# Graph sum and expert layers on one core: whole jobs behind a pair's sums, more scratch banks, biases in SBUF

## The chip, the core and the metric

The kernel runs on one core of a Trainium2 chip, in fp32. The metric is the time of one execution on the device in microseconds, as the median of several. Before the change the median of three runs is 2438.28 us (2429.11 to 2442.33).

## What is computed

The inputs are 12500 nodes of 256 features, and 200000 edges, each with a source, a destination and a weight, sorted by destination. Destinations are drawn as 12500 u^2, so low node numbers get many more edges than high ones.

```python
def _L0_gnn_ref(X, edge_src, edge_dst, edge_val, W, b):
    support = X @ W
    msgs = support[edge_src] * edge_val[:, None]
    out = jax.ops.segment_sum(msgs, edge_dst, num_segments=N_NODES)
    return out + b
...
h = jax.nn.gelu(jnp.einsum('nd,edf->enf', xf, W1) + b1[:, None, :], approximate=False)
y = jnp.einsum('enf,efd->end', h, W2) + b2[:, None, :]
out = jnp.einsum('ne,end->nd', w_dense, y)
out = _layer_norm(out + x, gamma, beta)
...
x = x + _L0_gnn_ref(_layernorm(x, axis=-1), src, dst, edge_weight, L0_gnn_W, L0_gnn_b)
x = x + _L0_ffn_ref(_layernorm(x, axis=-1)[None], L0_ffn_Wr, L0_ffn_br, L0_ffn_W1, L0_ffn_b1, L0_ffn_W2, L0_ffn_b2, L0_ffn_gamma, L0_ffn_beta)[0]
```

The router's logits come from the mean of the normalised rows over all tokens. So one softmax picks two of eight experts for the whole graph, with 256 x 512 and 512 x 256 weights each.

## The kernel before

**Start (0 to 96 us).** Rows of x are normalised and written to a DRAM table xn. The accumulator acc, which holds the summed messages of all nodes with features on the partitions, is cleared in SBUF.

**The pair loop (L898 to L933).** Edges are cut into chunks of 128 and these into groups of four. A pair is two such groups: eight chunks, 1024 edges. The loop runs over 180 pairs from high node numbers to low ones. For each pair:

- `gather_pair` (L480) issues eight indirect DMAs from POOL, one a chunk; each brings 128 rows of xn into a tile g. There are three such tiles. The gathers of pair i+1 are issued in iteration i, behind its products.
- `multiply` (L494) has a small TensorE product (L502) that waits for the gathers, and eight products of a chunk's rows with a weighted selection of 32 columns (L507). They fill one PSUM bank, pt; its pool has one. ACT copies it to SBUF, part (L510).
- `spread_out` (L515) runs one pair later: four products per pair (L522, two per group) put the sums of 32 columns on their places within a window of nodes, into the one bank ps, and DVE adds each group into acc at a place read from memory (L541).
- `select` (L437) makes the selections on DVE: for the first pairs in three instructions with two SBUF inputs (L462, L468, L472), later with a scalar form (L448).
- `prepare_segment` (L314) now and then turns the edges of the next segment into columns and places, with a few row products (L335).

**Dense part.** The first 128 chunks, those of the lowest nodes, are not gathered. In the pairs 1 to 44 `dense_make` (L602) makes two one-hot matrices for each of three chunks a pair on DVE, and `dense_add` (L612) multiplies them on TensorE (L620): products of one lot (four chunks, later two) sum up in one PSUM bank dps, then DVE adds the lot into a matrix inside acc (L634). There are 44 lots, and dps has one bank. Then `multiply_tiles` (L656) multiplies this matrix with xn, read in large tiles, in the same bank across nine pairs (L662); `place_dense` (L666) and `clear_matrix` (L675) put the result in place.

**Node blocks.** When all edges of a block of 256 nodes are in, `product` (L722) adds the graph's bias to the rows of x (L726, DVE), multiplies acc by W (L730, bank gz), adds both (L731) and takes the statistics; one pair later ACT normalises (L745), the next pair `transposed` (L754) transposes the rows (L759, again bank gz), ACT copies them out (L763), and DVE adds the last bias beta to acc (L768); then they are stored (`keep`). There are 49 blocks. Both biases lie in a PSUM bank of their own, bias_ps, filled at the start by a matmul (L297).

**Jobs.** A block and one of the two experts make a job, 98 in all. The first expert is named when 24 blocks are through, the second at 38. `job_steps` (L842) cuts a job: four first products (`first` L819, two matmuls of L822 each, into one of two banks ph, with Gelu by ACT L823) and two second products (`second` L825, four matmuls of L830 each, bank po, moved out by DVE L836). After every second `first` comes one `second` of the job before. `work` (L869) takes steps while a budget is above zero; a first costs 0.88, a second 1.75, and the budget of a pair starts from 10.0 - 2.5 - 1.0 (L915 to L918):

```python
budget = min(budget, 0.0) + PAIR_US - OWN_US - SLACK_US
budget -= 1.9 * complete + 1.3 * (stage_t is not None)
if i + 1 < len(pairs):
    budget = work(budget)
```

The order on every engine is that of the program, written by hand: on TensorE in one iteration the segment's rows, the pair's sums, the spread of the pair before, the dense steps, the job steps, transposes, product. On ACT the copy of the sums stands ahead of the Gelus of its iteration.

**Tail (2265 to 2447 us).** The last two jobs, then the two experts' outputs are mixed on TensorE (L1027, L1028), added and normalised for 25 double blocks. Mixes rotate through banks (`banks` L1009): three of their own, gz, the bias bank, and, when no jobs are left, ph and po.

Of the kernel before, what the change touches and what calls it, by code (L numbers as in the profile page):

```python
# [10 lines left out]
FP = mybir.dt.float32  # L11
# [3 lines left out]
ALU = mybir.AluOpType  # L15
# [3 lines left out]
P = 128  # L19
# [33 lines left out]
MARGIN = 8  # L53

PAIR_US = 10.0
OWN_US = 2.5
SLACK_US = 1.0

# [49 lines left out]
def gnn_ffn_kernel(  # L108
# [154 lines left out]
    jobs_stack, stack = ExitStack(), ExitStack()  # L263
    with tc.tile_pool(name="rt", bufs=1) as rt, tc.tile_pool(
        name="bias_ps", bufs=1, space=bass.MemoryType.PSUM
    ) as biasp, jobs_stack, stack, tc.manual_schedule():

# [13 lines left out]
        sp = open_pool(jobs_stack, name="small", bufs=4)  # L281
        gps, hps, ops = psum("gz_ps", 1, jobs_stack), psum("h_ps", 2, jobs_stack), psum("o_ps", 1, jobs_stack)

# [7 lines left out]

        bias_ps = biasp.tile([P, 2, D], FP, name="bias_ps")
        with tc.tile_pool(name="once", bufs=1) as once:
            bias_row = once.tile([1, 2, D], FP, name="bias_row")
            nc.scalar.dma_start(bias_row[:, 0], b_gnn[None, :])
            nc.scalar.dma_start(bias_row[:, 1], beta[None, :])
            nc.tensor.matmul(  # L297
                bias_ps.rearrange("p k d -> p (k d)"), row, bias_row.rearrange("p k d -> p (k d)"), start=True, stop=True
            )
        edgep = open_pool(name="edges", bufs=2)  # L300
# [118 lines left out]
        xp = open_pool(name="xrows", bufs=2)  # L419
        pps, aps, dps = psum("part_ps", 1), psum("agg_ps", 1), psum("dense_ps", 1)  # L420
        dp = open_pool(name="dense", bufs=1)
# [72 lines left out]
        def multiply(i, g):  # L494

            n = pairs[i][1]
            sel = selections[i][0]
            pt = pps.tile([P, GB, D], FP, name="pt")
            part = partp.tile([P, GB, D], FP, name="part")


            nc.tensor.matmul(  # L502
                pt[:NARROW, 0, : n * SUPER], sel[:, n * SUPER - 1], g[:, : n * SUPER, 0], start=True, stop=True
            )
            for j in range(n * SUPER):
                q = slice(j % SUPER * NARROW, (j % SUPER + 1) * NARROW)
                nc.tensor.matmul(  # L507
                    pt[q, j // SUPER], sel[:, j], g[:, j], start=True, stop=True, tile_position=(0, j % SUPER * NARROW)
                )
            nc.scalar.activation(part[:, :n], pt[:, :n], AF.Copy)  # L510
            return part

# [41 lines left out]
        dense_w = dp.tile([P, DENSE_CHUNKS], FP, name="dense_w")  # L554
        lot_i = dp.tile([1, len(lots)], I32, name="lot_i")

        def prepare_dense():
# [53 lines left out]

        def dense_add(c):  # L612

            g = next(g for g, (c0, k) in enumerate(lots) if c0 <= c < c0 + k)
            c0, k = lots[g]
            if c == c0:
                made["ps"] = dps.tile([P, 2 * D], FP, name="dps")
            ps = made["ps"][:, :QW]
            r, q = made.pop(c)
            nc.tensor.matmul(ps, r, q, start=(c == c0), stop=(c == c0 + k - 1))  # L620
            if c == c0 + k - 1:
# [12 lines left out]
                nc.vector.tensor_tensor(  # L634
                    at, at, ps.rearrange("p (h q n) -> p h q n", h=H, n=DENSE_WIN), ALU.add
                )
# [18 lines left out]

        def multiply_tiles(k):  # L656
            if k == 0:
                made["sum"] = dps.tile([P, 2 * D], FP, name="dps")
            for q in range(4 * k, min(4 * k + 4, NQ)):
                m = min(P, N - q * P)  # L660
                h, at = divmod(q, QH)
                nc.tensor.matmul(  # L662
                    made["sum"][:DENSE, :D], matrix[:m, h, at], loaded[k][:m, q % 4], start=(q == 0), stop=(q == NQ - 1)
                )

        def place_dense():  # L666

            by_node = w2_flat[:DENSE, :D]
            nc.scalar.activation(by_node, made["sum"][:DENSE, :D], AF.Copy)
            ps = dps.tile([P, H, 2 * P], FP, name="dps")  # L670
            for h in range(H):
                nc.tensor.transpose(ps[:, h, :DENSE], by_node[:, h * P : (h + 1) * P], ident[:DENSE, :DENSE])
            made["ps"] = ps

        def clear_matrix(i, n):  # L675
            w = QH * DENSE // n
            nc.vector.memset(acc[:, :, i * w : (i + 1) * w], 0.0)
            if i == 0:
                nc.scalar.activation(acc[:, :, :DENSE], made["ps"][:, :, :DENSE], AF.Copy)

        made_to = [0, 0]

        def dense_steps(i):

            if i == 0:
                prepare_dense()
                return
            while made_to[1] < made_to[0]:
                dense_add(made_to[1])
                made_to[1] += 1  # L690
            while made_to[0] < min(DENSE_CHUNKS, DENSE_STEP * i):
# [6 lines left out]
            if 0 <= k and ROWS_STEP * k < NLOAD:  # L698
                for j in range(ROWS_STEP * k, min(NLOAD, ROWS_STEP * k + ROWS_STEP)):
                    multiply_tiles(j)  # L700
                    load_tiles()
            if i == dense_pairs - 1:
                place_dense()
            if dense_pairs <= i < dense_pairs + 4:
# [49 lines left out]
        def transposed(b, z):  # L754

            ps = gps.tile([P, H, TB], FP, name="gz")
            for j in range(TPB):
# [8 lines left out]
            at = nodes(b * TPB, TPB)  # L766
            last_bias = halves(bias_ps[:, 1]).unsqueeze(1).to_broadcast([P, TPB, H, P])
            nc.vector.tensor_tensor(at, at, last_bias, ALU.add)  # L768
# [73 lines left out]
        def job_steps():  # L842

            while True:
                fetch()
                if not at_hand:
                    if behind:
                        yield 1.75, behind.pop(0)
                    else:
                        yield None  # L850
                    continue
                k, b, zT = at_hand.pop(0)
                fetch()
                hT = hp.tile([P, FC, TB], FP, name="hT")
                job_open[0] = True
                for c in range(FC):
                    yield 0.88, lambda c=c: first(k, zT, hT, c)
                    if c % 2 and behind:
                        yield 1.75, behind.pop(0)
                made = {}  # L860
                job_open[0] = False
                behind.extend(
                    [lambda h=h, a=(k, b, zT, hT, made): second(*a, h) for h in range(H)]
                )

        steps = job_steps()
        ready, named = [], 0

        def work(budget):  # L869

            while budget > 0:
                step = next(steps)
                if step is None:
                    break
                step[1]()
                budget -= step[0]
            return budget

# [19 lines left out]
        for i, (s0, n) in enumerate(pairs):  # L898
            k, at = seg_of(s0)
            since = 0 if at + n == segs[k][1] else since + 1  # L900
            if k + 1 < NSEG:
                if since == 0 and k > 0:
                    load_segment(k + 1)
                if since == 4:
                    prepare_segment(k + 1)
            part = multiply(i, g)
            if i + 1 < len(pairs):
# [101 lines left out]
        def banks():  # L1009
# [323 lines left out]
```

## Time and profile before

| what | value |
|---|---|
| median of three runs | 2438.28 us |
| profiled execution, its time | 2448.85 us |
| its span | 2446.9 us |
| granted TensorE clock, mean | 0.876 |
| TensorE busy | 1718.6 us, 70% |
| DVE busy | 1190.5 us, 49% |
| ACT busy | 475.8 us, 19% |
| POOL busy | 1488.0 us, 61% |
| gathers (L486) | 1436, 953 ns each |
| stretches | 0 to 96 start, 96 to 892 pairs with the dense part, 892 to 2265 pairs with jobs, 2265 to 2447 tail |

A line of the groups reads: line, engine, operation, output tile <- input tiles, size, count, then busy time and mean of one in ns, then the idle time of the engine just ahead of such instructions and what ended it. A line of a timeline reads: start in us, duration, engine, line, operation, tiles, count, and in brackets the idle time before it and its releaser. "issue" means that the trace shows nothing that it waited for, "remote" that the releaser is not known. PE is TensorE and PEld its weight loads. Matmul ends are modelled. The stretches above come from the table of engines by stretch.

### The profile page before, as it was taken

How to read it: one execution, taken by the hardware profiler on the slowest of the kernel's cores; microseconds unless marked ns; L12 is line 12 of the kernel's file. 1: busy time of each engine (PE TensorE's matmuls, PEld its weight loads, DVE VectorE, ACT ScalarE, POOL GpSimd, SP SyncE). 2: the span in 40 equal slices, each digit the busy share in tenths (PEclk: the TensorE clock that was granted, in tenths of full speed). 3: DMA queues.
4: the chain of work that ended last, by engine and by line, in shares of the span. 5: the costliest groups of instructions: out<-in, count | busy, mean ns of one | idle time of the engine just before them, and what ended most of it. 6: DMA issues, size and time to landing. Idle time of an engine off the chain costs nothing.

```text
span 2446.9 us, 29786 instructions
## 1 busy us (share of the span) xinstructions
PE 1718.6 (70%) x9698; PEld 1215.8 (50%) x9698; DVE 1190.5 (49%) x4265; ACT 475.8 (19%) x1085; POOL 1488.0 (61%) x1537
## 2 busy tenths in 40 slices
PE   0056655666567468888888878888887888888775
PEld 0033333333344246656656656566565665565675
DVE  7355555655533544545444444434433433343688
ACT  5201101111101122212122112212121211211233
POOL 5666656665565666666666666666666666665144
PEclk9987767877788779999999989999998999989898
DMA  8533333332375344444444454444444444444486
GB/s 304 193 91 116 103 93 102 109 114 83 116 225 167 110 145 142 136 138 139 141 131 135 138 151 144 133 134 141 133 136 125 137 137 134 130 123 120 160 281 219
DMA packets 167602, 349.17 MB, mean 143 GB/s; under 512 B 33514, under 2 KB 77072, under 8 KB 167440
## 3 DMA queue, kind: packets, MB, share of 16 engines
q0 software_dynamic: 68928, 188.31, 27.2%
q1 hardware_dynamic: 94120, 145.65, 17.6%
q10 hardware_dynamic: 4392, 13.21, 1.4%
q8 instruction: 82, 1.34, 0.2%
q14 instruction: 80, 0.66, 0.1%
HBM read 282.91 MB, written 64.14 MB: 142 GB/s over the span
## 4 chain that ended last, share of the span: by engine, by line
PE 48%; another core or an unknown queue 17%; DVE 16%; issue 12%; ACT 4%; DMA 2%; POOL 1%; SPq 0%; ACTq 0%; DVEq 0%; POOLq 0%
PE ph L822 14%; PE po L830 12%; PE ps L522 5%; PE pt L507 5%; PE dps L620 4%; PE gz L730 3%; DVE st L69 2%; PE dps L662 2%; DVE acc L541 1%; ACT hT L823 1%; ACT xt L393 1%; ACT part L510 1%; DVE nmt L1052 1%; DVE w L609 1%
## 5 line engine op out<-in xcount | busy, mean ns | idle before, releaser
L486 POOL DMA_INDIRECT g<-xn,src_i x1436 | 1368.3, 953 | 810.4 <-issue 394.2
L822 PE MATMUL ph<-zTj,w 128*128 128x256 f32 x1568 | 452.0, 420 | 127.5 <-issue 55.0
L830 PE MATMUL po<-hT,w 128*128 128x256 f32 x1568 | 438.3, 412 | 105.9 <-issue 80.9
L541 DVE TENSOR_TENSOR acc<-acc,ps 128x256 f32 x359 | 151.0, 421 | 678.8 <-remote 293.2
L822 PEld LDWEIGHTS ph<-zTj,w 128*128 128x128 f32 x1568 | 309.9, 208 | 229.0 <-issue 101.7
L830 PEld LDWEIGHTS po<-hT,w 128*128 128x128 f32 x1568 | 314.8, 206 | 197.6 <-issue 125.7
L510 ACT ACTIVATE part<-pt 128x512 f32<-128x512 f32 (+1 forms) x180 | 107.2, 596 | 1145.2 <-remote 596.2
L620 PE MATMUL dps<-w 128*128 128x490 f32 x256 | 151.5, 718 | 146.3 <-DVE acc L634 113.7
L823 ACT ACTIVATE hT<-ph,b 128x256 f32<-128x256 f32 x392 | 178.6, 472 | 311.2 <-PE ph L822 173.2
L448 DVE TENSOR_SCALAR sel<-iota,rel,wgt 128x32 f32<-128x32 f32 x992 | 233.4, 319 | 0.0
L522 PEld LDWEIGHTS ps<-spread,part 128*128 128x128 f32 x1436 | 186.8, 203 | 93.6 <-issue 87.0
L522 PE MATMUL ps<-spread,part 128*128 128x128 f32 x1436 | 223.3, 301 | 11.4 <-DVE acc L541 8.8
L507 PE MATMUL pt<-g,sel 128*32 128x256 f32 x2872 | 219.9, 418 | 0.0
L836 DVE SCALAR_TENSOR_TENSOR yT<-po,b,zTj 128x256 f32<-128x256 f32 x196 | 85.7, 479 | 163.1 <-PE po L830 73.5
L730 PE MATMUL gz<-wg,acc 128*128 128x256 f32 x392 | 120.0, 460 | 49.0 <-remote 15.2
L620 PEld LDWEIGHTS dps<-w 128*128 128x128 f32 x256 | 52.5, 232 | 203.6 <-DVE acc L634 133.8
L502 PE MATMUL pt<-g,sel 128*32 128x8 f32 (+1 forms) x360 | 42.4, 190 | 131.3 <-DMA g<-xn,src_i 71.6
L502 PEld LDWEIGHTS pt<-g,sel 128*32 128x32 f32 x360 | 26.2, 113 | 204.1 <-issue 165.2
L730 PEld LDWEIGHTS gz<-wg,acc 128*128 128x128 f32 x392 | 89.3, 233 | 74.3 <-issue 37.1
L731 DVE TENSOR_TENSOR acc<-gz,xt 128x512 f32<-128x512 f32 x49 | 33.9, 691 | 167.7 <-PE gz L730 107.1
L507 PEld LDWEIGHTS pt<-g,sel 128*32 128x32 f32 x2872 | 98.7, 118 | 26.2 <-issue 8.8
L1044 POOL TENSOR_TENSOR rst<-vet,half 128x4 f32<-128x4 f32 (+1 forms) x25 | 42.4, 1697 | 108.4 <-DVE vet L1042 108.4
(183 smaller groups left out, 1586.6 us busy)
## 6 DMA issues: line engine op xcount, KB each, us to landing
zTj<-zts SPq DMA_DIRECT2D x98, 256.0 KB
yts<-yT SPq DMA_DIRECT2D x98, 256.0 KB
ab<-yts SPq DMA_DIRECT2D x48, 512.0 KB
g<-xn,src_i POOLq DMA_INDIRECT x1436
zts<-zT SPq DMA_DIRECT2D x49, 256.0 KB
xt<-in_x SPq DMA_DIRECT2D x24, 512.0 KB
xn<-xt ACTq DMA_DIRECT2D x24, 512.0 KB
xt<-in_x SPq DMA_DIRECT2D x48, 256.0 KB
```

The lines of the kernel that those rows point to most:

```text
L448: nc.vector.tensor_scalar(sel[:, j * SUPER + c], iota[:, :NARROW], t["rel"][:, col], t["wgt"][:, col], ALU.is_equal, ALU.mult,)
L486: nc.gpsimd.indirect_dma_start(out=g[:, j], out_offset=None, in_=xn, in_offset=bass.IndirectOffsetOnAxis(ap=segment[k]["src_i"][:, col : c ...
L507: nc.tensor.matmul(pt[q, j // SUPER], sel[:, j], g[:, j], start=True, stop=True, tile_position=(0, j % SUPER * NARROW))
L510: nc.scalar.activation(part[:, :n], pt[:, :n], AF.Copy)
L522: nc.tensor.matmul(ps[:, j, h], part[:, j, h * P : (h + 1) * P], spread[:, j], start=True, stop=True)
L541: nc.vector.tensor_tensor(at, at, ps[:, j], ALU.add)
L620: nc.tensor.matmul(ps, r, q, start=(c == c0), stop=(c == c0 + k - 1))
L730: nc.tensor.matmul(ps[:, j], node_tile(t0 + j)[:, h], wg[:, h], start=(h == 0), stop=(h == H - 1))
L822: nc.tensor.matmul(ph, w1[:, k, h, c * P : (c + 1) * P], zT[:, h], start=(h == 0), stop=(h == H - 1))
L823: nc.scalar.activation(hT[:, c], ph, AF.Gelu, bias=b1[:, k, c : c + 1])
L830: nc.tensor.matmul(po[:, h], w2[:, k, c, h * P : (h + 1) * P], hT[:, c], start=(c == 0), stop=(c == FC - 1))
L836: nc.vector.scalar_tensor_tensor(yT[:, i], po[:, i], b2[:, k, i : i + 1], zT[:, i], op0=ALU.add, op1=ALU.add)
```

## The change

Six things are edited:

1. The copy of the sums leaves `multiply` and becomes `hand_over`, which is called behind the pair's job steps. Everything between is unchanged in order, so ACT now has the Gelus of an iteration ahead of its copy.
2. A pair gets a whole job or none: `work` starts one only with a budget above 3.5, and then does all of it. The seconds of the job before come first, then the four firsts. The budget is carried on unclipped, at 10.0 - 2.4 - 0.8 a pair.
3. The scratch pool h_ps has four banks in place of two. The bias bank and the dense bank are given up.
4. `dense_add` takes the chunks of a pair: the part of a lot that falls in a pair is summed in a scratch bank and added by DVE at once. This makes 72 pieces of 44 lots. `multiply_tiles` likewise sums one pair's tiles in a scratch bank, and DVE copies or adds it to an SBUF tile by_node. The transpose moves from `place_dense` to the first step of `clear_matrix`. Block transposes use a scratch bank as well.
5. The biases lie in an SBUF tile, loaded by two broadcasting DMAs on ACT's queue; L726 and L768 read it in place of PSUM.
6. The tail's mixes have two banks of their own, and the rotation uses scratch banks where the third and the bias bank were.

Both kernels do 384 first and 192 second products within the pair loop (96 jobs) and two jobs behind it. In the changed order about 97 of the pairs 62 to 177 have a whole job behind their sums and some 20 have none.

```diff
 PAIR_US = 10.0
-OWN_US = 2.5
-SLACK_US = 1.0
+OWN_US = 2.4
+SLACK_US = 0.8
+JOB_US = 3.5
...
-        gps, hps, ops = psum("gz_ps", 1, jobs_stack), psum("h_ps", 2, jobs_stack), psum("o_ps", 1, jobs_stack)
+        gps, hps, ops = psum("gz_ps", 1, jobs_stack), psum("h_ps", 4, jobs_stack), psum("o_ps", 1, jobs_stack)
...
+        biases = rt.tile([P, 2, D], FP, name="biases")
+        for k, v in enumerate((b_gnn, beta)):
+            nc.scalar.dma_start(biases[:, k], bass.AP(tensor=v.tensor, offset=v.offset, ap=[[0, P], [1, D]]))
...
-        pps, aps, dps = psum("part_ps", 1), psum("agg_ps", 1), psum("dense_ps", 1)
+        pps, aps = psum("part_ps", 1), psum("agg_ps", 1)
...
+            return part, pt
+
+        def hand_over(i, part, pt):
+            n = pairs[i][1]
             nc.scalar.activation(part[:, :n], pt[:, :n], AF.Copy)
-            return part
...
+        def dense_add(c0, c1):
+
+            for g, (a, k) in enumerate(lots):
+                b0, b1 = max(a, c0), min(a + k, c1)
+                if b0 >= b1:
+                    continue
+                ps = scratch_ps()[:, :QW]
+                for c in range(b0, b1):
+                    r, q = made.pop(c)
+                    nc.tensor.matmul(ps, r, q, start=(c == b0), stop=(c == b1 - 1))
...
-            nc.vector.tensor_tensor(xt, xt, bias_ps[:, 0].unsqueeze(1).to_broadcast([P, TPB, D]), ALU.add)
+            nc.vector.tensor_tensor(xt, xt, biases[:, 0].unsqueeze(1).to_broadcast([P, TPB, D]), ALU.add)
...
-            ps = gps.tile([P, H, TB], FP, name="gz")
+            ps = scratch_ps().rearrange("p (h t) -> p h t", h=H)
...
+                while behind:
+                    yield 1.75, behind.pop(0), False
                 for c in range(FC):
...
+                    yield 0.88, lambda c=c: first(k, zT, hT, c), c == FC - 1
...
-            while budget > 0:
+            while budget > least:
...
+                while least and not step[2]:
+                    step = next(steps)
+                    step[1]()
+                    budget -= step[0]
...
-            budget = min(budget, 0.0) + PAIR_US - OWN_US - SLACK_US
+            budget += PAIR_US - OWN_US - SLACK_US
             budget -= 1.9 * complete + 1.3 * (stage_t is not None)
             if i + 1 < len(pairs):
-                budget = work(budget)
+                budget = work(budget, JOB_US)
+            hand_over(i, part, pt)
...
-        mps = psum("mix_ps", 3)
+        mps = psum("mix_ps", 2)
...
-                yield from (m, z, m, lambda: bias_ps, m) if jobs_left() else (m, h, z, m, h, lambda: bias_ps, m, o)
+                yield from (m, h, z, m, h) if jobs_left() else (m, h, z, h, m, h, o, h)
```

More of the change, by code (lines that the diff above doesn't have):

```diff
@@ L263, in gnn_ffn_kernel @@
     jobs_stack, stack = ExitStack(), ExitStack()
-    with tc.tile_pool(name="rt", bufs=1) as rt, tc.tile_pool(
-        name="bias_ps", bufs=1, space=bass.MemoryType.PSUM
-    ) as biasp, jobs_stack, stack, tc.manual_schedule():
+    with tc.tile_pool(name="rt", bufs=1) as rt, jobs_stack, stack, tc.manual_schedule():
         def open_pool(on=stack, **k):
@@ L290, in gnn_ffn_kernel @@
         sumc = rt.tile([P, H, NBLK], FP, name="sumc")
[L292 to L299, printed above, removed]
+        biases = rt.tile([P, 2, D], FP, name="biases")
+        for k, v in enumerate((b_gnn, beta)):
+            nc.scalar.dma_start(biases[:, k], bass.AP(tensor=v.tensor, offset=v.offset, ap=[[0, P], [1, D]]))
         edgep = open_pool(name="edges", bufs=2)
@@ L555, in gnn_ffn_kernel @@
         lot_i = dp.tile([1, len(lots)], I32, name="lot_i")
+        by_node = dp.tile([DENSE, D], FP, name="by_node")
         def prepare_dense():
@@ L610, in dense_make @@
             made[c] = (r, q)
[L612 to L621, printed above, removed]
+        def dense_add(c0, c1):
[7 more added lines that the diff above has]
+                    nc.tensor.matmul(ps, r, q, start=(c == b0), stop=(c == b1 - 1))
                 if g not in lot_regs:
@@ L654, in load_tiles, with multiply_tiles @@
             loaded.append(t)
[L656 to L659, printed above, removed]
+        def multiply_tiles(k0, k1):
+            ps = scratch_ps()[:DENSE, :D]
+            q0, q1 = 4 * k0, min(4 * k1, NQ)
+            for q in range(q0, q1):
                 m = min(P, N - q * P)
@@ L662, in multiply_tiles @@
                 nc.tensor.matmul(
-                    made["sum"][:DENSE, :D], matrix[:m, h, at], loaded[k][:m, q % 4], start=(q == 0), stop=(q == NQ - 1)
+                    ps, matrix[:m, h, at], loaded[q // 4][:m, q % 4], start=(q == q0), stop=(q == q1 - 1)
                 )
[L666 to L673, printed above, removed]
+            if k0 == 0:
+                nc.vector.tensor_copy(by_node, ps)
+            else:
+                nc.vector.tensor_tensor(by_node, by_node, ps, ALU.add)
         def clear_matrix(i, n):
@@ L678, in clear_matrix @@
             if i == 0:
-                nc.scalar.activation(acc[:, :, :DENSE], made["ps"][:, :, :DENSE], AF.Copy)
+                ps = scratch_ps().rearrange("p (h n) -> p h n", h=H)
+                for h in range(H):
+                    nc.tensor.transpose(ps[:, h, :DENSE], by_node[:, h * P : (h + 1) * P], ident[:DENSE, :DENSE])
+                nc.scalar.activation(acc[:, :, :DENSE], ps[:, :, :DENSE], AF.Copy)
         made_to = [0, 0]
@@ L687, in dense_steps @@
                 return
-            while made_to[1] < made_to[0]:
-                dense_add(made_to[1])
-                made_to[1] += 1
+            dense_add(made_to[1], made_to[0])
+            made_to[1] = made_to[0]
             while made_to[0] < min(DENSE_CHUNKS, DENSE_STEP * i):
@@ L698, in dense_steps @@
             if 0 <= k and ROWS_STEP * k < NLOAD:
-                for j in range(ROWS_STEP * k, min(NLOAD, ROWS_STEP * k + ROWS_STEP)):
-                    multiply_tiles(j)
+                k0, k1 = ROWS_STEP * k, min(NLOAD, ROWS_STEP * k + ROWS_STEP)
+                multiply_tiles(k0, k1)
+                for _ in range(k0, k1):
                     load_tiles()
-            if i == dense_pairs - 1:
-                place_dense()
             if dense_pairs <= i < dense_pairs + 4:
@@ L766, in transposed @@
             at = nodes(b * TPB, TPB)
-            last_bias = halves(bias_ps[:, 1]).unsqueeze(1).to_broadcast([P, TPB, H, P])
+            last_bias = halves(biases[:, 1]).unsqueeze(1).to_broadcast([P, TPB, H, P])
             nc.vector.tensor_tensor(at, at, last_bias, ALU.add)
@@ L847, in job_steps @@
                     if behind:
-                        yield 1.75, behind.pop(0)
+                        yield 1.75, behind.pop(0), not behind
                     else:
@@ L855, in job_steps, with work @@
                 job_open[0] = True
+                while behind:
+                    yield 1.75, behind.pop(0), False
                 for c in range(FC):
[L857 to L864, printed above, removed]
+                    job_open[0] = c < FC - 1
+                    if not job_open[0]:
+                        made = {}
+                        behind.extend(
+                            [lambda h=h, a=(k, b, zT, hT, made): second(*a, h) for h in range(H)]
+                        )
+                    yield 0.88, lambda c=c: first(k, zT, hT, c), c == FC - 1
         steps = job_steps()
         ready, named = [], 0
-        def work(budget):
-            while budget > 0:
+        def work(budget, least=0.0):
+            while budget > least:
                 step = next(steps)
                 if step is None:
-                    break
+                    return min(budget, 0.0)
                 step[1]()
                 budget -= step[0]
+                while least and not step[2]:
+                    step = next(steps)
+                    step[1]()
+                    budget -= step[0]
             return budget
@@ L905, in gnn_ffn_kernel @@
                     prepare_segment(k + 1)
-            part = multiply(i, g)
+            part, pt = multiply(i, g)
             if i + 1 < len(pairs):
```

## Prediction

> **What bounds the kernel now.** I read the table of engines by stretch first, then the three timelines of one pair side by side, then the groups and a pair that breaks the pattern. Columns of the table: stretch, its length, busy time of PE, PEld, DVE, ACT and POOL, granted clock, DMA share, GB/s.
>
> ```profile
> 96.00:892.00 796.00, 454.75 (x2381) 266.11 (x2380) 409.05 (x1353) 84.68 (x215) 491.69 (x511) 0.78 0.40 119
> 892.00:2265.00 1373.00, 1134.33 (x6418) 832.07 (x6418) 578.39 (x2265) 281.86 (x653) 870.56 (x920) 0.92 0.45 136
> 2265.00:2447.00 182.00, 125.19 (x892) 115.92 (x884) 140.91 (x361) 56.73 (x118) 70.19 (x37) 0.87 0.66 221
> ```
>
> The pairs with jobs (892 to 2265) hold 1373 us of 2447, and TensorE is busy for 83% of them. That looks like a bound; it is not. The copy of a pair's sums (ACT L510) and the gathers (POOL L486) show what beats the time:
>
> ```profile
> 975.10 0.60 ACT L510 ACTIVATE part<-pt 128x512 f32<-128x512 f32 x1 [4.37 <-PE ph L822]
> 986.91 0.60 ACT L510 ACTIVATE part<-pt 128x512 f32<-128x512 f32 x1 [7.10 <-PE ph L822]
> 998.74 0.60 ACT L510 ACTIVATE part<-pt 128x512 f32<-128x512 f32 x1 [8.01 <-remote]
> ```
>
> ```profile
> 984.03 0.95 POOL L486 DMA_INDIRECT g<-xn,src_i  x1 [0.30 <-issue]
> 987.09 0.94 POOL L486 DMA_INDIRECT g<-xn,src_i  x1 [2.11 <-PE ph L822]
> ...
> 995.83 0.95 POOL L486 DMA_INDIRECT g<-xn,src_i  x1 [0.30 <-issue]
> 998.91 0.94 POOL L486 DMA_INDIRECT g<-xn,src_i  x1 [2.14 <-remote]
> ```
>
> ```profile
> 981.03 1.03 PE L507 MATMUL pt<-g,sel 128*32 128x256 f32 x13
> 982.00 1.16 PE L522 MATMUL ps<-spread,part 128*128 128x128 f32 x8
> 982.99 1.03 PE L822 MATMUL ph<-zTj,w 128*128 128x256 f32 x4
> 983.86 1.89 PE L830 MATMUL po<-hT,w 128*128 128x256 f32 x8
> 985.58 1.03 PE L822 MATMUL ph<-zTj,w 128*128 128x256 f32 x4
> ```
>
> The copies stand 11.81 and 11.83 us apart. The sums start near 981.0, yet their copy starts at 986.91: 2.88 us after 984.03, the start of the last gather issued. TensorE streamed everything behind the sums without a wait meanwhile, so the sums are held by the gathers in flight and not by the queue behind them. The release lets POOL start the gathers three pairs on (g has three buffers): eight starts 1.25 us apart (8.75), 2.88 to the release, 0.2 to the next start: 11.83. It is a ring of POOL, DMA and the sums. Pair 110 (all engines' timeline) came late, when its last gather, started at 1458.21, was no longer in flight:
>
> ```profile
> 1461.31 0.20 PE L502 MATMUL pt<-g,sel 128*32 128x8 f32 x1
> ...
> 1462.58 0.60 ACT L510 ACTIVATE part<-pt 128x512 f32<-128x512 f32 x1 [1.05 <-PE pt L507]
> ```
>
> Its copy starts 1.27 us after its sums. Over the 115 pairs from 892 on the copies span 1368.5 us, 11.90 a pair: all but 0.07 is ring. Between one copy and the next pair's sums lie 2.5 to 7.5 us; the ring only lengthens if the sums start later than about 11.83 - 1.3 = 10.5 us after the copy before. TensorE's load per pair is free up to there.
>
> Before 892 the ring is the same but is broken more often: 730 us for 58 pairs, 12.59 each, so 0.76 x 58 = 44 us above it.
>
> ```profile
> L620 PE MATMUL dps<-w 128*128 128x490 f32 x256 | 151.5, 718 | 146.3 <-DVE acc L634 113.7
> ```
>
> **The change part by part,** against the profiled execution's 2448.85 us, which is 10.6 over the median of 2438.28.
>
> *Dense pieces in scratch banks.* The one dense bank made TensorE wait 113.7 us for DVE's add. Most of it lay under the ring. What the ring did not hide is how late a pair's release came after its last gather, over 2.88: pair 13 9.8 - 2.88 = 6.9, pair 17 4.2, pair 22 4.4, pair 28 2.7, pair 43 5.8, together 24.0 us; in each the wait on L634 came ahead of the sums. Pairs 20 and 36 lose 7.7 and 13.4 more, but segment rows and DVE end last there, so I take none. With four banks these waits go: -24. Next in line is the ring. The change adds 28 DVE adds (44 become 72 at 0.67 us: 18.7 us) where DVE works 409 of 796 us: hidden behind the ring, or at worst spending the whole gain again. Bounds -45 to +5. The tiles' sum (L662) waited 36.3 us on DVE L541, which stays, since the reader of the cleared matrix is the same.
>
> *Sums that start at once.* Where sums started 0.65 us after the copy before, two pairs took 23.1 to 23.7 us, not 23.7: at most 0.6 for two. With TensorE unblocked in the first 62 pairs, a third of 29 such twos: -6 (0 to -15).
>
> *Whole jobs, copy last.* Same 384 first and 192 second products before the last pair as before; what moves is their place: about 97 pairs carry a whole job, 20 none. Behind the sums TensorE has spread 1.0, two seconds 3.5, four firsts 3.5, with no bank or ACT wait between them (four banks, last job's hT is done). ACT's order becomes four gelus (L823, 0.47 each), then the copy (0.60). The price is on the link from release to next sums, since pt has one bank. When the release comes (up to 9.3 us behind the sums' start by this period) the records of about half of the eight microseconds have passed: about 3.9 left, then the last gelu 0.47, copy 0.60, hand-offs 0.4: the next sums start 5.4 us behind the release, 7.3 where a product (L730, 1.89) lies between. Both are under 10.5, so cost 0. If no record counts before the release: 8.0 + 1.5 = 9.5, and 11.4 with a product, over the limit. If the cover is gone the price is that excess times its pairs. The gathers three pairs on wait for the sums, not for the copy, so they are queued behind nothing new on POOL; DVE's adds (L541) of the next pair wait on the copy, and transposes and normalised rows on ACT are queued behind it, a few us late with 11.8 to do it in. The hold-ups of before in this part (about 8 us, pairs 110, 111, 146, 175) may go or be joined by others: 0, bounds -8 to +45.
>
> *Biases in SBUF.* DVE's 98 adds (L726 and L768, 0.68 us, 49 each) get a second SBUF input, beside gathers on POOL. The row: where DVE's selections with two SBUF inputs (L462, L468, L472; 0.42 us) overlap a gather, its spacing is 1.347 us on average against 1.25, +0.097. 98 x 0.097 = 9.5, nearly all on the ring: +9. The Trainium skill (SBUF — State Buffer, "SBUF: two separate sides") speaks against this edit: a DVE operation with two SBUF inputs and a GpSimd operation that reads SBUF exclude each other for a whole instruction. By the rule I would add up to 98 x 0.68 = 67 us and forecast a loss; the row shows a seventh of that, and it decides. Bounds 0 to +20.
>
> The same section says that TensorE never waits for DMAs on the other side of SBUF. By that, sums would come 1.27 us after their start as at pair 110, no ring would exist, and whole jobs would be worth what TensorE's order is worth. The trace holds the sums of 981.0 until 986.91, 5.9 us, with gathers in flight; I follow it.
>
> *Tail and prologue.* In the tail DVE is busy for 140.9 of 182 us. Mixes go from three own banks and the bias bank to two own and more scratch; beta's last add reads SBUF. Near rows: DVE with two SBUF inputs takes 1.22 ns an element (L1068, 1250 ns for 1024), with PSUM 1.32 (676 for 512). +2, bounds -3 to +8. Ahead of the pairs one matmul of under a microsecond becomes two broadcast loads on ACT's queue while POOL and DMA set the pace: 0 (-2 to +2); the first reader is hundreds of us later.
>
> Sum: -24 - 6 + 0 + 9 + 2 + 0 = -19. 2448.85 - 19 = 2429.9 for an execution like the profiled one, 2438.3 - 19 = 2419 for the median.
>
> **The rivals.**
> *Main case (0.45)*: as summed, 2384 to 2428.
> *R1, no change (0.27)*: 28 more DVE adds and the gathers' spacing spend what the dense banks give. -24 + 19 + 9 + 2 - 6 = 0: 2438. For it: every period is 11.8 whatever TensorE does. Against it: the five pairs' losses stand beside a wait that goes.
> *R2, slower (0.20)*: TensorE's results behind the sums count only from the release on, so the copy behind the fourth gelu starts 9 us late and the next sums pass 10.5. It decides from there. At a period of 12.5 instead of 11.85 on 96 whole-job pairs: 96 x 0.65 = 62, so 2438 + 62 = 2500. For it: copy and gelus at 986.91 to 989.28 came in a row, which could mean that nothing behind the sums counted earlier. Against it: the firsts' four gelus would need only 0.47 each behind such a burst, unless TensorE itself stands still.
> *R3, the change frees the sums (0.08)*: sums are held by whatever waits behind them on TensorE; with nothing waiting they are released at once and POOL runs unbroken, 8 x 1.25 = 10.0 a pair: 115 x 1.85 = 213, so about 2225. Against it: at 981 to 987 nothing waited, and the sums were held all the same.
>
> **How the numbers follow.** This kernel's measurement can tell about 0.5%, 12 us, from no change: faster is below 2426, slower above 2450. Of the main case 0.42 lies below 2426 and 0.03 above; of R1 0.24 lies within and 0.03 above 2450 (28 hidden adds that don't hide); R2 is above, R3 far below. Faster 0.42 + 0.08 = 0.50, same 0.03 + 0.24 = 0.27, slower 0.03 + 0.20 = 0.23. The main case and R1 reach from 2384 to about 2457; a mild R2 (a period of 12.2: 96 x 0.35 = 34, 2472) takes the range to 2470. R3 and the worse part of R2, about 0.2, stay out.
>
> **What would show it.** Right: L510 still 11.8 to 11.9 apart after 892, each 2.9 after the last gather's start, with 12.2 or less a pair before 892 and the wait on L634 near nothing; sums starting 5 to 7.5 us behind the release. R2: sums over 10 us behind it and periods of 12.5. R3: POOL's 2.1 us gap gone and gathers 1.25 us apart across pairs. Gather spacing of 1.9 us where a bias add runs would show the exclusive lock. I am wrong first if the hold on the sums is not the gathers' doing.

## The result, and the profile after

The changed kernel takes 2639.36 us (median of four, 2632.56 to 2647.67) beside 2433.7 us of the kernel before: a ratio of 1.0843, 95% interval 1.0794 to 1.0893. It is 206 us slower where 19 us less were forecast. The profiled execution has a span of 2636.3 us, 189.4 more than before.

The starts of the copies of the sums (L510 before, L509 after) divide these 189.4 us. Up to pair 61 the changed kernel is 35.2 us ahead (845.0 against 880.2 us). From pair 61 to 177 it takes 1601.8 us instead of 1380.3, 221.5 more. From there to the end it takes 189.5 instead of 186.4. The whole loss arises in the pairs with jobs. The table of engines by stretch after the change, columns as before:

```profile
96.00:892.00 796.00, 463.04 (x2466) 283.26 (x2466) 435.54 (x1410) 90.63 (x229) 523.79 (x526) 0.79 0.41 123
892.00:2265.00 1373.00, 999.21 (x5570) 789.10 (x5569) 512.25 (x2000) 242.56 (x573) 757.22 (x793) 0.84 0.39 119
```

In the same 1373 us every engine does less than before: TensorE 999 us against 1134, POOL 757 against 871. TensorE's granted clock is 0.84 instead of 0.92. No engine became the bound; a chain of waits grew. The groups of the page name its links:

```profile
L481 POOL DMA_INDIRECT g<-xn,src_i x1436 | 1393.5, 970 | 977.1 <-PE pt L502 468.2
...
L497 PE MATMUL pt<-g,sel 128*32 128x8 f32 (+1 forms) x360 | 44.6, 197 | 572.4 <-ACT part L509 379.4
L819 ACT ACTIVATE hT<-ph,b 128x256 f32<-128x256 f32 x392 | 178.8, 473 | 1246.9 <-PE ph L818 554.8
...
L620 PE MATMUL ph<-w 128*128 128x490 f32 x256 | 136.2, 673 | 28.6 <-DVE w L608 25.5
```

The same groups before the change:

```profile
L486 POOL DMA_INDIRECT g<-xn,src_i x1436 | 1368.3, 953 | 810.4 <-issue 394.2 <-remote 177.7 <-PE pt L507 100.3
...
L823 ACT ACTIVATE hT<-ph,b 128x256 f32<-128x256 f32 x392 | 178.6, 472 | 311.2 <-PE ph L822 173.2 <-issue 49.7 <-remote 35.6
...
L502 PE MATMUL pt<-g,sel 128*32 128x8 f32 (+1 forms) x360 | 42.4, 190 | 131.3 <-DMA g<-xn,src_i 71.6 <-ACT part L510 33.3 <-issue 26.4
```

Read backwards: POOL waits for the sums, the sums for ACT's copy (379 us against 33 before), ACT for first products (555 against 173 us). The last line of the first block answers the dense wait: 146.3 us of idle time ahead of L620 became 28.6, and L634 is gone from it. One pair in order of time, TensorE, ACT, then POOL:

```profile
1060.52 0.20 PE L497 MATMUL pt<-g,sel 128*32 128x8 f32 x1 [2.87 <-ACT part L509]
...
1063.02 4.83 PE L826 MATMUL po<-hT,w 128*128 128x256 f32 x16
1067.69 3.62 PE L818 MATMUL ph<-zTj,w 128*128 128x256 f32 x16
1071.14 1.89 PE L726 MATMUL gz<-wg,acc 128*128 128x256 f32 x8
1074.27 0.20 PE L497 MATMUL pt<-g,sel 128*32 128x8 f32 x1 [1.24 <-ACT part L509]
```

```profile
1068.81 0.47 ACT L819 ACTIVATE hT<-ph,b 128x256 f32<-128x256 f32 x1 [8.34 <-PE po L826]
1069.62 0.47 ACT L819 ACTIVATE hT<-ph,b 128x256 f32<-128x256 f32 x1 [0.33 <-issue]
1071.82 0.47 ACT L819 ACTIVATE hT<-ph,b 128x256 f32<-128x256 f32 x1 [1.73 <-PE ph L818]
1073.25 0.47 ACT L819 ACTIVATE hT<-ph,b 128x256 f32<-128x256 f32 x1 [0.96 <-PE gz L726]
1073.62 0.59 ACT L509 ACTIVATE part<-pt 128x512 f32<-128x512 f32 x1
```

```profile
1061.96 0.94 POOL L481 DMA_INDIRECT g<-xn,src_i  x1 [4.36 <-PE pt L502]
...
1070.70 0.95 POOL L481 DMA_INDIRECT g<-xn,src_i  x1 [0.30 <-issue]
1075.70 0.94 POOL L481 DMA_INDIRECT g<-xn,src_i  x1 [4.05 <-PE pt L502]
```

The sums start at 1060.52 with no gather in flight and release the gathers 1.4 us later. Now it is the first products that are held. All four end by 1071.3 on TensorE's records. Two Gelus follow at once; the third and fourth start at 1071.82 and 1073.25, the last one 2.55 us behind the start of the last gather. (The trace names the product L726 as the fourth's releaser; in pairs without a product the fourth Gelu is just as late, as the table of four pairs below shows.) Behind it stand the copy and, for the copy, the next sums at 1074.27. So what ran side by side now runs in a row: 8.75 us of gathers, 2.55 to the last release, 1.0 for Gelu, copy and hand-offs, 1.4 for the sums, 13.7 in all. Where the trace records half the TensorE clock, the release comes 2.3 us behind the start of the sums, and the row is 14.6. Of the 74 pairs from 62 to 177 whose sums started with no gather in flight, 53 were at half clock (2.34 us in the median) and 21 at full clock (1.44 us).

### The profile page after: what moved, and what is told of

It reads as the page before. It is cut to its first block, busy times and chain, and to the rows that moved or that the text cites. A ratio compares the mean times of both kernels' runs of the same rounds, so it can differ in the third digit from the quotient of the medians.

```text
span 2636.3 us, 29807 instructions
## 1 busy us (share of the span) xinstructions
PE 1723.7 (65%) x9696; PEld 1295.0 (49%) x9696; DVE 1214.5 (46%) x4302; ACT 471.3 (18%) x1084; POOL 1513.2 (57%) x1537
## 5 line engine op out<-in xcount | busy, mean ns | idle before, releaser
L481 POOL DMA_INDIRECT g<-xn,src_i x1436 | 1393.5, 970 | 977.1 <-PE pt L502 468.2
L826 PE MATMUL po<-hT,w 128*128 128x256 f32 x1568 | 388.4, 404 | 0.3 <-issue 0.3
L818 PE MATMUL ph<-zTj,w 128*128 128x256 f32 x1568 | 361.3, 383 | 22.4 <-issue 14.1
L497 PEld LDWEIGHTS pt<-g,sel 128*32 128x32 f32 x360 | 28.5, 123 | 643.9 <-ACT part L509 431.2
L520 PEld LDWEIGHTS ps<-spread,part 128*128 128x128 f32 x1436 | 254.3, 265 | 170.0 <-issue 158.6
L520 PE MATMUL ps<-spread,part 128*128 128x128 f32 x1436 | 298.9, 369 | 56.6 <-DVE acc L539 33.7
L818 PEld LDWEIGHTS ph<-zTj,w 128*128 128x128 f32 x1568 | 301.0, 192 | 65.5 <-issue 15.6
L502 PE MATMUL pt<-g,sel 128*32 128x256 f32 x2872 | 280.9, 508 | 3.4 <-issue 3.3
L509 ACT ACTIVATE part<-pt 128x512 f32<-128x512 f32 (+1 forms) x180 | 106.9, 594 | 384.0 <-remote 206.5
L620 PE MATMUL ph<-w 128*128 128x490 f32 x256 | 136.2, 673 | 28.6 <-DVE w L608 25.5
L726 PE MATMUL gz<-wg,acc 128*128 128x256 f32 x392 | 116.2, 447 | 55.0 <-DVE acc L539 32.6
L502 PEld LDWEIGHTS pt<-g,sel 128*32 128x32 f32 x2872 | 116.5, 134 | 42.1 <-issue 29.8
L726 PEld LDWEIGHTS gz<-wg,acc 128*128 128x128 f32 x392 | 84.6, 223 | 77.8 <-DVE acc L539 35.0
L620 PEld LDWEIGHTS ph<-w 128*128 128x128 f32 x256 | 54.6, 230 | 82.1 <-issue 39.0
```

The source lines that it names most:

```text
L481: nc.gpsimd.indirect_dma_start(out=g[:, j], out_offset=None, in_=xn, in_offset=bass.IndirectOffsetOnAxis(ap=segment[k]["src_i"][:, col : c ...
L502: nc.tensor.matmul(pt[q, j // SUPER], sel[:, j], g[:, j], start=True, stop=True, tile_position=(0, j % SUPER * NARROW))
L520: nc.tensor.matmul(ps[:, j, h], part[:, j, h * P : (h + 1) * P], spread[:, j], start=True, stop=True)
L620: nc.tensor.matmul(ps, r, q, start=(c == b0), stop=(c == b1 - 1))
L726: nc.tensor.matmul(ps[:, j], node_tile(t0 + j)[:, h], wg[:, h], start=(h == 0), stop=(h == H - 1))
L818: nc.tensor.matmul(ph, w1[:, k, h, c * P : (c + 1) * P], zT[:, h], start=(h == 0), stop=(h == H - 1))
```

## The experiments

The runs fell on chips of two kinds. On the one kind (call them holding chips: chips 2, 11 and 15, and the chip of the measurement above, whose number is not on record) the kernel before takes 2428 to 2449 us. On the other (chips 4, 9 and 10) it takes 2087 to 2089 us, the same code. So ratios to the kernel before on the same chip are compared. Each numbered chip was met once, so whether a chip stays of its kind is not shown.

**The changed kernel again, and the copy alone moved back** (holding chip)

```diff
             part, pt = multiply(i, g)
+            hand_over(i, part, pt)
...
-            hand_over(i, part, pt)
```

> The changed kernel itself once more, since the four runs before it came from a chip on which the kernel before takes 2087 us and holds no sums. If this chip holds the sums behind gathers (the kernel before near 2434 us), 2639 us; if it does not, POOL runs unbroken, the copy's place costs nothing, and the time is within 10 us of the variant with the copy first, 2105 us.

> The changed kernel with the copy ahead of the job steps, on the same chip as the run above. On a chip that holds the sums: theory (the copy behind held Gelus) 2400 us with a period of 11.85 us; rival (the clump of TensorE work makes the pair long) near 2600 us. On a chip that does not: 2105 us again.

2670.93 us (1.0886, 1.0857 to 1.0916) and 2435.08 us (0.994, 0.9917 to 0.9964). With whole jobs, the place of one ACT instruction is worth the whole loss; with the copy ahead of them, whole jobs and their clump of eight microseconds leave the pairs 62 to 177 at 11.91 us each, as before (11.90). The rival "clump" falls.

**The copy last in the kernel before**

```diff
-            nc.scalar.activation(part[:, :n], pt[:, :n], AF.Copy)
...
                 budget = work(budget)
+            hand_over(i, part, pt)
```

> The kernel before with nothing changed but the copy moved behind the job steps. On a chip that holds TensorE's results behind gathers (the kernel before near 2440 us): theory (the copy behind held Gelus) says job pairs of 13 to 14.6 us and 2560 to 2650 us; the rival (only a whole job in a clump lengthens the pair) says no change, 2440. On a chip that doesn't: 2088 us again.

2443.31 us, 1.0074 (1.0042 to 1.0105). My theory as I had put it falls here: the copy's place alone is worth 0.7%, not 8%. Both edits are needed; the next runs and one table bear on why.

**The copy one and two Gelus earlier**

```diff
         def first(k, zT, hT, c):
+            if c == 2:
+                flush()
...
```

Here `flush` makes the pending copy, so it stands between the second and third Gelu; with `c == 3`, one Gelu earlier than in the changed kernel, it stands between the third and fourth.

> The changed kernel with the copy between the second and third Gelu of a job, again for a chip that holds (the kernel before near 2440 us). Theory (limit for the next sums): period near 11.9 us, 2430 to 2460 us. If the price grows evenly with the copy's place: about 2550. On a chip that doesn't hold, 2108 again.

2432.14 us, 1.0009 (0.9986 to 1.0032). The loss does not fall evenly with the place of the copy: two Gelus take all of it away. The timelines of TensorE and ACT in this kernel show a copy that slipped in ahead of a held Gelu:

```profile
1103.99 3.62 PE L826 MATMUL ph<-zTj,w 128*128 128x256 f32 x16
1107.44 0.60 PE L755 MATMUL ph<-ident,z 128*128 128x128 f32 x4
1107.97 0.20 PE L497 MATMUL pt<-g,sel 128*32 128x8 f32 x1
```

```profile
1105.11 0.47 ACT L827 ACTIVATE hT<-ph,b 128x256 f32<-128x256 f32 x1 [4.07 <-PE ph L826]
1105.92 0.47 ACT L827 ACTIVATE hT<-ph,b 128x256 f32<-128x256 f32 x1 [0.33 <-PE ph L826]
1106.29 0.59 ACT L509 ACTIVATE part<-pt 128x512 f32<-128x512 f32 x1
1107.03 0.47 ACT L827 ACTIVATE hT<-ph,b 128x256 f32<-128x256 f32 x1
1111.28 0.47 ACT L827 ACTIVATE hT<-ph,b 128x256 f32<-128x256 f32 x1 [3.78 <-PE ps L520]
```

The fourth first ends at 1107.61 and its Gelu starts at 1111.28, 3.7 us later; the next sums had started at 1107.97.

The table is worked out from the starts of POOL's and TensorE's rows in the traces of holding chips between 900 and 2230 us: how far behind a pair's first gather the next sums start, and how long it then is to the next pair's first gather (pairs with no gap over 2.6 us within their eight gathers; single values or ranges where only a few pairs fall in a column, else medians).

| kernel | next sums, median | pairs over 10.5 us | period, sums at 4 to 10.5 | at 10.5 to 11.5 | at 11.5 to 14 |
|---|---|---|---|---|---|
| before | 4.5 | 3 of 112 | 11.9 | | 13.3 to 14.7 |
| copy last only | 5.0 | 10 of 110 | 11.7 | 12.3 to 13.4 | 13.1 to 15.1 |
| whole jobs, copy first | 5.9 | 3 of 111 | 11.9 | | 15.5 |
| copy behind two Gelus | 5.7 | 9 of 111 | 11.8 | 12.5, 13.4 | 15.7 to 16.0 |
| changed | 12.3 | 74 of 96 | 11.6 | 12.4 | 14.7 |

In all of them the median period is below 12 us up to 10.5 and longer past it; outside the changed kernel this rests on a few pairs. The copy behind old job steps stays inside the limit most of the time; behind four Gelus of a whole job it does not.

Why two Gelus are enough is seen when each Gelu of a job is set against the modelled end of its first. In the changed kernel (same stretch) 13 of 81 first Gelus start more than 1 us late, 35 of 81 second, 61 of 82 third and 80 of 82 fourth ones. Lateness in the series of gathers is not the reason by itself: with whole jobs and the copy first, of the firsts that end 3.5 to 6 us behind a series' start, none of 64 first and second ones has a late Gelu, and 42 of 47 fourth ones have. Why the last results of a clump are held and the first are not stays open.

**A second bank for the sums** (copy last, and copy first)

```diff
-        gps, hps, ops = psum("gz_ps", 1, jobs_stack), psum("h_ps", 4, jobs_stack), psum("o_ps", 1, jobs_stack)
+        gps, hps, ops = psum("gz_ps", 1, jobs_stack), psum("h_ps", 3, jobs_stack), psum("o_ps", 1, jobs_stack)
...
-        pps, aps = psum("part_ps", 1), psum("agg_ps", 1)
+        pps, aps = psum("part_ps", 2), psum("agg_ps", 1)
```

> The changed kernel, copy last, but two PSUM banks for the sums (scratch pool three). On a holding chip: theory says that what hurts is only the next sums' wait for the copy, so 2435 us or less; two pairs' sums can then be released together, two periods in 8.75 x 2 + 1.25 + 3.1 = 21.9 us, and 115 pairs would save up to 105 us against the copy-first variant, 2330. If the clump itself is the cause: 2600. On the other chip: 2107 us again.

> Two sum banks and the copy ahead of the job steps. On a holding chip: as the run above or better, 2330 us, if two pairs' sums are released together; 2435 us if each pair's sums still bring one release. On the other chip 2105 us.

2454.86 us (1.0135, 1.0089 to 1.0181) and 2422.96 us (0.9969, 0.9943 to 0.9996). With the copy still last, a second bank takes most of the loss away (31 of 109 pairs still lie past 10.5 us), so the sums' wait for the copy is the link. The hoped-for release of two pairs at once did not come: the median period stays 12.1 and 11.7 us. Why the second pair's sums are not released with the first's is open.

**No gathers from pair 62 on**

```diff
-                g = gather_pair(i + 1)
+                g = gather_pair(i + 1) if i + 1 < 62 else g
```

> The kernel before without the gathers of the pairs from 62 on: their sums use the rows of pair 61, so this part of the output is left out. If the gathers are what holds TensorE's results, the sums of these pairs come about 1.2 us after their start, and the 115 pairs run at TensorE's own pace, 8.7 to 10 us each: 2080 to 2250 us on a holding chip. If the hold is a property of TensorE's order there, the period stays at 11.85 and the time near 2440. On the other chip TensorE's pace, 8.7 to 9.8 us instead of 10, and so 1960 to 2085 us.

88351.23 us. The time as a whole says nothing: with other sums the routing changes, and a fallback behind the loop runs for 86 ms. The pair loop itself can be read. Copies of pairs 62 to 177 span 1013.5 us, 8.81 a pair against 11.90, with the same jobs done. Where ACT was idle, the copy starts 0.15 us (median; at most 0.42) behind the modelled end of the sums, and every one of 384 Gelus starts within 0.10 us of the end of its first or of ACT's instruction before it, on chip 15, where the old kernel with the copy last and both kernels with two banks were held. TensorE first, then ACT:

```profile
1214.29 1.03 PE L507 MATMUL pt<-g,sel 128*32 128x256 f32 x13
1215.24 1.16 PE L522 MATMUL ps<-spread,part 128*128 128x128 f32 x8
```

```profile
1215.46 0.60 ACT L510 ACTIVATE part<-pt 128x512 f32<-128x512 f32 x1 [2.78 <-PE pt L507]
```

So it is the gathers that hold TensorE's results; its order alone does not. Whether it is POOL's issuing of them or the transfers that follow is not separated by this run.

**On the other kind of chip**

> Theory (copy behind held Gelus): in the changed kernel the sums start 2.8 us behind the release because ACT's copy stands behind Gelus whose first products are held by the gathers; with the copy back ahead of the job steps and all else as changed, the period of job pairs returns from 14.6 to 11.85 us, and with the 35 us gained in the dense part the time is about 2400 us. Rival (clump of TensorE work): eight us of job work in one pair make the pair long by themselves; then the period stays near 14 and the time near 2600.

> The copy stays last, but the sums have two PSUM banks and the scratch pool three. Theory: the next sums no longer wait for the copy, so the period is 11.9 to 12.5 us and the time 2400 to 2460. Rival (clump of TensorE work): 2600 as before.

> Dense pieces, scratch banks, SBUF biases and tail as changed, but the job order, budgets and the place of the copy as before. Theory: the dense part's 35 us remain and nothing else, about 2403 us. Rival (SBUF biases slow the gathers by an exclusive lock): up to 67 us of it are lost again, 2440 to 2470.

> The kernel before with nothing changed but the copy moved behind the job steps. Theory: the place of the copy alone lengthens job pairs to about 14 us and the time to about 2650. Rival (clump of TensorE work): job steps are spread as before, so no change, 2438.

> The changed kernel with the copy between the second and third Gelu of a job. On a holding chip (the kernel before near 2440 us): in the changed kernel the second Gelu starts 6.5 to 8 us behind the first gather, ahead of the held ones, so the copy is through at about 8.5 us, and the next sums start as TensorE ends its firsts, 9.3 us behind the release and ahead of the 10.5 us limit. Theory (limit): period near 11.9 us, 2430 to 2460 us. If the price grows evenly with the copy's place: half of it, about 2550. On the other chip 2105.

> The copy between the third and fourth Gelu. On a holding chip the third Gelu starts 7.4 to 11.3 us behind the first gather, some of them held; theory: pairs on both sides of the limit, 2500 to 2580 us. If only the fourth Gelu matters: 2440. On the other chip 2105.

> The copy between the third and fourth Gelu, on a holding chip. The third Gelu starts 7.4 to 11.3 us behind the first gather in the changed kernel, some of them held. Theory: pairs on both sides of the limit, 2450 to 2550 us; 2432 if only the fourth Gelu is ever held long enough. On a chip that doesn't hold, 2111 again.

Ratios are 1.0093, 1.0107, 1.0109, 1.0005, 1.0094, 1.0100 and 1.0083 (each to within 0.002), times 2088 us for the old kernel with the copy last and 2105 to 2111 for the rest. Expectations written for holding chips are not answered by these; how much the copy between third and fourth Gelu costs on a holding chip was not measured, nor was the changed kernel itself on this kind. POOL of the old kernel with the copy last shows what differs:

```profile
1212.66 0.95 POOL L486 DMA_INDIRECT g<-xn,src_i  x1 [0.30 <-issue]
1213.91 0.95 POOL L486 DMA_INDIRECT g<-xn,src_i  x1 [0.30 <-issue]
1215.16 0.94 POOL L486 DMA_INDIRECT g<-xn,src_i  x1 [0.30 <-issue]
```

Gathers follow each other 1.25 us apart across the pairs, 10.0 us a pair, and TensorE's results arrive beside them. ACT's copy at 1214.25 stands behind six Gelus, and POOL does not wait for it. Here POOL is the bound, and whatever has SBUF biases is 1% slower.

**The biases back in PSUM** (copy first; scratch pool three). First with whole jobs, then with the old job order, that is, the dense pieces alone:

```diff
-            nc.vector.tensor_tensor(xt, xt, biases[:, 0].unsqueeze(1).to_broadcast([P, TPB, D]), ALU.add)
+            nc.vector.tensor_tensor(xt, xt, bias_ps[:, 0].unsqueeze(1).to_broadcast([P, TPB, D]), ALU.add)
...
```

> Copy first, whole jobs, dense pieces, but the biases back in a PSUM bank and three scratch banks. Gathers took 25 us more in all with SBUF biases (970 against 953 ns, 1436 of them). If these lie on the ring: 2435 - 20 = 2415 us on a holding chip and 2085 on the other; if not, 2435 and 2105.

> Copy first, whole jobs, dense pieces, biases in a PSUM bank, three scratch banks, again for a holding chip: 2415 us if the 20 us that the SBUF biases cost on the other chip lie on the ring as well; 2435 if not. On a chip that doesn't hold, 2088 again.

> The dense pieces alone: old job order, copy first, biases in PSUM, three scratch banks, tail as changed. On a holding chip the 35 us of the dense part stay whole: 2440 - 33 = 2407 us. On the other chip, where POOL's unbroken gathers set the pace, 2085 to 2090.

> The dense pieces alone, with the job order of before, the copy first, biases in PSUM and three scratch banks, on a holding chip. If the 35 us of the dense part stay to the end: a ratio of 0.985, about 2400 us. If the job part gives most of it back, as in the copy-first variants: 0.995, about 2420. On a chip that doesn't hold, 2089 again.

On the other kind of chip 2087.87 (0.9994), 2089.14 (1.0001) and 2089.51 us (1.0005): the 1% is the biases', about 20 us, and not the scratch pool's, since two sum banks with SBUF biases also had a pool of three and took 1.0107. On a holding chip (chip 2) 2420.06 us (0.9959, 0.9928 to 0.999); the same kernel with SBUF biases had 0.994 (0.9917 to 0.9964) on chip 11, so no cost of them shows, though the intervals leave room for some microseconds. The dense pieces alone were not measured on a holding chip. This kernel, with whole jobs, the copy first and biases in PSUM, is the one version measured on both kinds that is slower on neither; its 0.4% gain is below the 0.5% that the prediction took as measurable.

How biases in SBUF lengthen a gather, from the timeline of all engines in the kernel with old jobs and SBUF biases:

```profile
247.02 2.18 POOL L481 DMA_INDIRECT g<-xn,src_i  x1 [0.30 <-issue]
247.09 0.68 DVE L764 TENSOR_TENSOR acc<-acc,biases 128x512 f32<-128x512 f32 x1
...
247.69 0.68 DVE L722 TENSOR_TENSOR xt<-xt,biases 128x512 f32<-128x512 f32 x1
```

Two adds back to back stretch one gather from 0.95 to 2.18 us. Over the whole trace of the changed kernel a gather takes 0.953 us where no bias add overlaps it, 1.14 where one does (89 gathers) and 1.71 where two or more do (11); before, with the biases in PSUM, it takes 0.95 to 0.97 in all three cases.

## Why the prediction was wrong, step by step

**The bound: right.** The ring of gathers, DMA and sums sets the pace on holding chips, and the limit of 10.5 us for the next sums is where the table has it.

**Dense pieces: right on holding chips.** The forecast was -24 and -6 us by pair 61; these two profiles show -35.2. Over all traces of holding chips the old dense code reaches pair 61 at 880.2, 852.6 and 864.4 us, the new one at 835.5 to 853.5 in seven, which is -21 between the means. The one profile that I worked from lies at the upper end in this stretch, so the ratio of 0.994 with the copy first, -14 us, need not mean a gain given back. On the other kind of chip nothing is gained: 719.7 us with the old code, 717.8 to 722.7 with the new one and biases in PSUM.

**Whole jobs, copy last: the step that failed.** It said that "the records of about half of the eight microseconds have passed" at the release, that the next sums start 5.4 us behind it and 7.3 with a product, and so "cost 0". The limit was right and the start was wrong: 12.3 us behind the first gather in the median. The sum took a first's result as there when TensorE's work ends. It weighed that results may count only from the release on (9.5 us), but not that the gathers which this release starts hold the last firsts in turn: the fourth Gelu starts 2.7 us (median) behind the end of its first. That hold makes the difference. In late pairs at full clock the fourth first ends 7.7 us behind the first gather, and from the fourth Gelu to the next sums it is 1.0 us. Without the hold the sums would start near 8.7 us where no product lies between (an estimate from these two figures), inside the limit. The trace of before showed little of this: of the firsts that end in the first five microseconds of a gather series, 35 of 180 have a Gelu more than 1 us late, and later ones stood behind a held copy anyway.

The start of 5 to 8 us that I forecast does exist, but it does not last. A run of four pairs in the changed kernel, from its timelines, us from the pair's first gather (own sums start ahead of it):

```
first gather   own sums   fourth first ends   fourth Gelu   next sums
1269.6         -5.6       6.55                6.59          7.61
1281.3         -4.1       4.96                7.12          8.13
1293.0         -3.6       7.20                8.50          9.52
1304.8         -2.3       6.86                11.39         12.41
```

Later sums leave the next pair less of a lead, and so its clump ends later in its series: the fourth first ends 9.1 us behind its own sums in the second and fourth pair, and 10.8 in the third, where the trace records half clock for 3.4 us. At the limit the gathers run dry, and then the row of 13.7 to 14.6 us repeats itself, with a lead of 1.4 or 2.3 us. 74 of 96 series lie past the limit (77 of 95 on chip 11). From pair 62 to 177 the mean period is 13.74 us: (13.74 - 11.90) x 115 = 212 us in place of 0, with a bound of +45. Of these, 53 x 0.9 = 48 us are the slower release at half clock, by estimate.

**R2 was the nearest rival, and too small.** Its place (the copy behind the fourth Gelu) and its point (10.5 us) are what the runs show. Its mechanism is not quite: results do not all count from the release on; the last ones are held again by the next gathers. Its price was an excess of 0.65 us a pair, 62 us. What happens past the limit is not a small excess: gathers, Gelu, copy and sums, which overlapped, come to stand in a row. The argument against it was that Gelus behind such a burst need only 0.47 us each; in the pair shown above the third and fourth start 1.43 us apart, each on its own.

**Biases in SBUF: +9 us forecast.** The gathers take 970 instead of 953 ns, 25 us in all. On the chips where POOL is the bound they cost about 20 us; on holding chips no cost shows. The row I took (0.42 us selections, +0.097 us) was too short a kind of operation: the 98 adds of 0.68 us cost the gathers 0.26 us each on average, and two in a row cost one gather 1.23 us. The Trainium skill's exclusive lock (SBUF — State Buffer, "SBUF: two separate sides") would have given 67; the measured 20 lies between. The 2.18 us row comes near its block of a whole instruction (1.23 us lost against 1.28 us of adds), though that gather had started ahead of the adds; most overlaps cost less.

**That TensorE never waits for DMAs** (the same section) is said of ports, and TensorE's own records do stream on. What the forecast drew from it, results on time beside gathers, holds in the traces of three chips and not on holding chips, where taking the gathers away freed the results. Whether a port has to do with it, no run here shows.

**Tail: right.** From the last copy to the end 181.0 us against 181.5.

**R1** did not come. **R3**'s period is what the other chips do with any order (10.0 us a pair), which no order of TensorE brought about.

## What to carry to other kernels

Find out in which part of its cycle a result is late, not only how long its work takes: a consumer that stands behind the last of several results inherits the worst of their delays. Where one bank is handed round, put the instruction that frees it ahead of work that can wait on the same engine. When a step is costed at nothing because it starts before a limit, ask what one pair past the limit does to the next: here each late start took lead from the next pair, and an overlap worth 1.9 to 2.8 us a pair was lost within four pairs.

## What the runs showed of the hardware

- Chips differ in kind. On holding chips TensorE's results can reach other engines late while gathers are in flight: the sums at 981.03 us before the change were copied at 986.91, and in the changed kernel the fourth Gelu of a job is 2.7 us late in the median. The last release comes 2.5 to 2.9 us behind the start of the last gather. On the three others, and without gathers on chip 15, copies and Gelus start 0.04 to 0.15 us (medians) behind the modelled end of what they read. The kernel before takes 2428 to 2449 us on the one kind and 2087 to 2089 us on the other. What causes it is not known from these runs.
- On holding chips the first results of a clump mostly pass between gathers and the last ones mostly do not (13 of 81 first and 80 of 82 fourth Gelus over 1 us late).
- The traces of holding chips record fewer semaphore updates: in the profile before 1618 of DVE's 2510 and 517 to 1081 on each of the gathers' semaphores, where the other kind (old kernel, copy last) records 2509 of 2510 and 2814 to 2879. Whether this is a loss of records or part of the hold stays open; every timed execution comes with readings of the profiler, so none shows the hold without recording.
- A gather on POOL that overlaps one DVE add of 0.68 us with two SBUF inputs takes 1.14 us in place of 0.953, and 1.71 with two or more; with one input in PSUM it stays at 0.95 to 0.97.
- The changed kernel's TensorE, which waits more, was granted a clock of 0.84 in its job pairs against 0.92, and its sums released the gathers after 2.34 us instead of 1.44 in the pairs where the clock was halved.
